# Pairwise products of fields: order of the pairs, PSUM operand, store sizes and the split of the last store

## The chip, the cores and the metric

The kernel runs on one core of one Trainium2 chip. The metric is the device time of one execution in microseconds (us); shorter is better. A profile shows one execution in detail; its span runs from the first to the last instruction of the program, and the device time includes a little on both sides of it.

## What is computed

```python
def ref(x, W):                      # x: (4096, 32, 64) float32, W: (64, 64) float32
    vid = einsum('bfd,de->bfe', x, W)
    idx_i, idx_j = triu_indices(32, k=1)
    return x[:, idx_i, :] * vid[:, idx_j, :]      # (4096, 496, 64)
```

For each of 4096 samples there are 32 fields of 64 numbers. Each field is multiplied by W, and each of the 496 pairs of fields i < j gives the elementwise product of field i as it came and field j after the multiplication. Input is 33.6 MB, output 520 MB, all float32.

## The kernel before, in words

The host lays x out as 16 tiles of shape 128 partitions x 32 fields x 128 samples: each of two groups of 128 samples takes 64 partitions, one for each of the 64 numbers. The output of a tile is 128 partitions x 496 pairs x 128 samples, so a pair is 512 bytes of a partition and 64 KB in all. The host puts the output into the reference's order afterwards.

For each tile, `project` (line 63) multiplies the fields by W on TensorE (line 72): a matmul takes four fields (one PSUM bank of 512 float32 columns) of one half of the partitions, and the compiler makes two instructions of each. ScalarE copies groups of eight fields from PSUM to an SBUF tile `vid` (line 79). `products` (line 82) walks over the left fields i: VectorE multiplies field i, broadcast, by the run of fields j after it (line 88). A tile's 496 pairs are cut into slots of 83 pairs (`SLOT`, line 34), with three slot buffers (line 46), and `store` (line 95) sends a slot to the output by a DMA on the queue of SP: six stores a tile, of which the last is 81 pairs. In tile 0 the pairs are made backwards, from the last left field, so that its first stores are small (lines 109 to 118): 10, 18, 27 and 26 pairs, then halves of slots.

Loads of x come in on SP for tiles 0 (four pieces of eight fields, last fields first) and 1 (two pieces of 16 fields). For later tiles they are four pieces on ScalarE's queue, called after a few stores of the tile before (lines 124 to 125). There are two x buffers, so the load of a tile waits until VectorE and TensorE have left the tile two earlier. W is loaded twice, once for each half of the partitions, on ScalarE's queue (lines 53 and 54). The order on SP is that of the program text; the framework adds the waits, and gives every DMA a semaphore that counts its landing.

Of the kernel before, what the change touches and what calls it, by code (L numbers as in the profile page):

```python
# [1 line left out]

# [4 lines left out]

F32 = mybir.dt.float32
ALU = mybir.AluOpType

P = 128

C = 128


@with_exitstack
def pairwise_bilinear_kernel(
    ctx: ExitStack,
    tc: tile.TileContext,
    x: bass.AP,  # L20
    w: bass.AP,
    out: bass.AP,
):

    nc = tc.nc
    NT, _, F, _ = x.shape
    D = P // 2
    NP = F * (F - 1) // 2

    GRP = 8  # L30
    NGRP = F // GRP
    BANK = 512 // C

    SLOT = 83
    AHEAD = 2
    PIECES = 4

    off = [i * (F - 1) - i * (i - 1) // 2 for i in range(F)]


    ctx.enter_context(tc.manual_schedule(engines={mybir.EngineType.SP}))

    const = ctx.enter_context(tc.tile_pool(name="const", bufs=1))
    xpool = ctx.enter_context(tc.tile_pool(name="x", bufs=AHEAD))
    vpool = ctx.enter_context(tc.tile_pool(name="vid", bufs=2))
    opool = ctx.enter_context(tc.tile_pool(name="out", bufs=3))
    psum = ctx.enter_context(
        tc.tile_pool(name="ps", bufs=4, space=bass.MemoryType.PSUM)
    )


    w2 = const.tile([P, D], F32)
    nc.scalar.dma_start(out=w2[0:D, :], in_=w)
    nc.scalar.dma_start(out=w2[D : 2 * D, :], in_=w)

    xs = {}

    def load(t, lo, hi, queue=nc.sync):
        if t not in xs:
            xs[t] = xpool.tile([P, F, C], F32, tag="x", name=f"x_{t}")  # L60
        queue.dma_start(out=xs[t][:, lo:hi, :], in_=x[t][:, lo:hi, :])

    def project(t, order):

        vid = vpool.tile([P, F, C], F32, tag="vid", name=f"vid_{t}")
        for g in order:
            pv = psum.tile([P, GRP, C], F32, tag="pv", name=f"pv_{t}_{g}")
            for b in range(0, GRP, BANK):
                f = g * GRP + b
                for h in range(2):  # L70
                    half = slice(h * D, (h + 1) * D)
                    nc.tensor.matmul(  # L72
                        pv[half, b : b + BANK, :],
                        lhsT=w2[half, :],
                        rhs=xs[t][half, f : f + BANK, :],
                        start=True,
                        stop=True,
                    )
            nc.scalar.copy(vid[:, g * GRP : (g + 1) * GRP, :], pv)  # L79
        return vid  # L80

    def products(t, vid, ot, base, a, b, backwards=False):

        fields = [i for i in range(F - 1) if off[i] < b and off[i + 1] > a]
        for i in reversed(fields) if backwards else fields:
            s, e = max(a, off[i]), min(b, off[i + 1])
            j = i + 1 + s - off[i]
            nc.vector.tensor_tensor(  # L88
                ot[:, s - base : e - base, :],
                xs[t][:, i : i + 1, :].to_broadcast([P, e - s, C]),  # L90
                vid[:, j : j + e - s, :],
                ALU.mult,
            )

    def store(t, ot, base, a, b):
        nc.sync.dma_start(out=out[t][:, a:b, :], in_=ot[:, a - base : b - base, :])


    for g in reversed(range(NGRP)):
        load(0, g * GRP, (g + 1) * GRP)  # L100
    load(1, F // 2, F)
    load(1, 0, F // 2)

    for t in range(NT):
        vid = project(t, reversed(range(NGRP)) if t == 0 else range(NGRP))
        bases = list(range(0, NP, SLOT))
        if t == 0:

            ends = [NP, off[27], off[24], off[21], bases[-1]]
            for n, base in enumerate(reversed(bases)):  # L110
                top = min(base + SLOT, NP)
                if n:
                    ends = [top, (base + top) // 2, base]
                ot = opool.tile([P, SLOT, C], F32, tag="o", name=f"o_{t}_{n}")
                for b, a in zip(ends, ends[1:]):
                    products(t, vid, ot, base, a, b, backwards=True)
                    store(t, ot, base, a, b)
        else:
            for n, base in enumerate(bases):
                top = min(base + SLOT, NP)  # L120
                ot = opool.tile([P, SLOT, C], F32, tag="o", name=f"o_{t}_{n}")
                products(t, vid, ot, base, base, top)
                store(t, ot, base, base, top)
                if 1 <= n <= PIECES and t + 1 < NT and t + 1 not in (0, 1):
                    load(t + 1, (n - 1) * F // PIECES, n * F // PIECES, nc.scalar)


_INS = ["r_x", "L0_rec_W"]
_OUTS = [((4096, 496, 64), "float32")]


# [28 lines left out]
```

## Time and profile before

| | |
|---|---|
| median of 4 runs | 1297.98 us (1297.72 to 1298.29) |
| the profiled execution's own time | 1297.76 us |
| its span | 1295.9 us |
| mean rate of the DMA over the span | 427 GB/s |
| HBM read, written | 33.59 MB, 520.09 MB |
| DMA engines' time taken by SP's queue, by ScalarE's | 93.9%, 5.6% |
| stores of 5312 KB: number, us from issue to landing | 75, 28.8 |
| x pieces of 512 KB on ScalarE's queue: number, us to landing | 56, 31.8 |
| TensorE clock granted, mean | 0.547 |

How to read it: PE is TensorE's matmuls and PEld its weight loads, DVE is VectorE, ACT is ScalarE, POOL is GpSimd, SP is SyncE. A group line gives source line, engine, operation, output and inputs, count, busy time and mean duration. In the rows of 40 slices a digit is the busy share in tenths of a 32 us slice. A row of a stretch gives, after its length, the busy time and count of PE, PEld, DVE, ACT and POOL, then the granted clock, the mean share in which the 16 DMA engines were busy, and GB/s. A line of waits gives who waited for whom, the total, the times and the longest, in us. A DMA is cut into packets, here one for each partition; each of the 16 engines works off its own share of them, and one of the landing counts is sent by each engine.

### The profile page before, as it was taken

What the parts mean: (1) busy time and instruction counts of PE and PEld (TensorE: products, weight loads), DVE (VectorE), ACT (ScalarE), POOL (GpSimd) and SP (SyncE); (2) the same over time, 40 slices, a digit from 0 to 9 for tenths busy, and PEclk for the clock granted to TensorE, in tenths of its full rate; (3) what the DMA queues carried; (4) which work ended last, traced back from release to release, by engine and by line L of the source; (5) the groups of instructions that cost most, each with busy time, mean ns of one, the idle gap of its engine ahead of it and who ended that gap; (6) DMA issues with size and microseconds to landing.
All of it is one profiled execution on the core that took longest, in us unless ns stands there. A gap on an engine that the chain in (4) does not pass through costs nothing.

```text
span 1295.9 us, 2185 instructions
## 1 busy us (share of the span) xinstructions
PE 217.4 (17%) x512; PEld 56.0 (4%) x512; DVE 1105.8 (85%) x581; ACT 66.1 (5%) x65; POOL 0.2 (0%) x4
## 2 busy tenths in 40 slices
PE   5013022120221302113031130311203122021000
PEld 2000000000000000000000000000000000000000
DVE  6999988889888888888888888888888888988991
ACT  2001000000000000000000000000000000000000
POOL 0000000000000000000000000000000000000000
PEclk9556566555555655556555555655556555565555
DMA  8999999999999999999999999999999999999997
GB/s 337 430 404 442 432 435 432 431 433 432 431 435 434 431 433 432 433 432 433 434 432 433 433 431 432 434 433 431 432 435 429 437 429 433 433 427 436 437 430 342
DMA packets 24076, 553.82 MB, mean 427 GB/s; under 512 B 2816, under 2 KB 2816, under 8 KB 10624
## 3 DMA queue, kind: packets, MB, share of 16 engines
q1 hardware_dynamic: 15840, 524.30, 93.9%
q10 hardware_dynamic: 8224, 29.40, 5.6%
q8 instruction: 4, 0.07, 0.0%
q14 instruction: 8, 0.07, 0.0%
HBM read 33.59 MB, written 520.09 MB: 427 GB/s over the span
## 4 chain that ended last, share of the span: by engine, by line
DMA 63%; DVE 33%; issue 1%; PE 0%; DVEq 0%; ACT 0%
DMA out_dram<-o 63%; DVE o L88 33%; DMA w<-in_L_rec_W_dram 0%; PE pv L72 0%; DVEq L154 0%; ACT vid L79 0%; DVEq L88 0%
## 5 line engine op out<-in xcount | busy, mean ns | idle before, releaser
L88 DVE TENSOR_TENSOR o<-x,vid 128x1408 f32<-128x1408 f32 (+15 forms) x581 | 1105.8, 1973 | 163.8 <-DMA out_dram<-o 152.9
L72 PE MATMUL pv<-x,w 64*64 64x512 f32 x512 | 217.4, 994 | 960.1 <-DMA x<-in_r_x_dram 954.8
L79 ACT COPY vid<-pv 128x1024 f32<-128x1024 f32 x64 | 64.8, 1012 | 1110.5 <-PE pv L72 998.7
L72 PEld LDWEIGHTS pv<-x,w 64*64 64x64 f32 x512 | 56.0, 204 | 1119.8 <-issue 1105.8
L79 ACT ACT_TABLE_LOAD x1 | 1.3, 1283 | 1.9 <-issue 1.9
L139 POOL MEMSET const-bfloat16-1.0<- 128x1 bf16 x1 | 0.1, 103 | 0.0
L139 POOL MEMSET const-uint8-127<- 128x1 uint8 x1 | 0.1, 102 | 0.0
L139 POOL MEMSET const-float32-0.0<- 128x1 f32 x1 | 0.1, 100 | 0.2 <-issue 0.2
L139 POOL MEMSET const-float32-1.0<- 128x1 f32 x1 | 0.1, 99 | 0.0
## 6 DMA issues: line engine op xcount, KB each, us to landing
out_dram<-o SPq DMA_DIRECT2D x75, 5312.0 KB, 28.8
out_dram<-o SPq DMA_DIRECT2D x15, 5184.0 KB, 27.7
x<-in_r_x_dram ACTq DMA_DIRECT2D x56, 512.0 KB, 31.8
out_dram<-o SPq DMA_DIRECT2D x5, 2688.0 KB, 10.2
out_dram<-o SPq DMA_DIRECT2D x5, 2624.0 KB, 10.8
x<-in_r_x_dram SPq DMA_DIRECT2D x4, 512.0 KB, 5.7
x<-in_r_x_dram SPq DMA_DIRECT2D x2, 1024.0 KB, 9.6
out_dram<-o SPq DMA_DIRECT2D x1, 1728.0 KB, 5.5
```

The source lines that it names most:

```text
L72: nc.tensor.matmul(pv[half, b : b + BANK, :], lhsT=w2[half, :], rhs=xs[t][half, f : f + BANK, :], start=True, stop=True,)
L79: nc.scalar.copy(vid[:, g * GRP : (g + 1) * GRP, :], pv)
L88: nc.vector.tensor_tensor(ot[:, s - base : e - base, :], xs[t][:, i : i + 1, :].to_broadcast([P, e - s, C]), vid[:, j : j + e - s, :], ALU ...
L139: nc = _bacc.Bacc("TRN2", target_bir_lowering=False, num_devices=1)
```

## The change

The order of the pairs, and with it the layout of the output in device memory, goes by right field: all pairs with j = 1, then j = 2, and so on; the pairs of a right field are consecutive (`first(j)` is where they start). The host's reordering follows. VectorE now multiplies a run of x fields by one right field, broadcast, and reads that field in PSUM, where the matmul left it. The copies by ScalarE and the tile `vid` in SBUF are gone. The eight PSUM banks hold the 32 fields of a tile, one bank for four fields.

A slot has 124 pairs, so that a tile has four; three buffers as before. A store goes out at the end of a slot, and over the first two tiles also at the sizes that `GROWING` lists: 26 stores that sum to 992 pairs. The last store of the last tile is cut by `steps`: first eight DMAs, each of 16 partitions, that leave out the last 1 to 8 pairs (one more for each group), then for each group two small DMAs for those pairs, one of 15 to 8 partitions and one of 1 to 8.

The host passes W already doubled, and one DMA on SP loads it before x. Tile 0 comes in four pieces, first fields first, tile 1 in two, later ones in four on ScalarE's queue, all called at the start of the tile before. The program is built with a smaller scratch area for DMA descriptors in SBUF (1024), which leaves room for the larger slots.

```diff
+SLOT = 124
+GROWING = [
+    21, 15, 19, 23, 27, 19, 29, 18, 19, 20, 38, 28, 24, 25, 47, 34, 29, 61,
+    55, 69, 66, 58, 77, 47, 93, 31,
+]
+def first(j):
+    return j * (j - 1) // 2
+def steps(lo, hi):
+    for g in range(8):
+        yield lo, hi - g - 1, 16 * g, 16 * g + 16
+    for g in range(8):
+        yield hi - g - 1, hi, 16 * g, 16 * g + 15 - g
+        yield hi - g - 1, hi, 16 * g + 15 - g, 16 * g + 16
...
-        tc.tile_pool(name="ps", bufs=4, space=bass.MemoryType.PSUM)
+        tc.tile_pool(name="ps", bufs=8, space=bass.MemoryType.PSUM)
...
-    nc.scalar.dma_start(out=w2[0:D, :], in_=w)
-    nc.scalar.dma_start(out=w2[D : 2 * D, :], in_=w)
+    nc.sync.dma_start(out=w2, in_=w)
...
+    def load(t, pieces, queue):
+        xt = xpool.tile([P, F, C], F32, tag="x", name=f"x_{t}")
+        n = F // pieces
+        for lo in range(0, F, n):
+            queue.dma_start(out=xt[:, lo : lo + n, :], in_=x[t][:, lo : lo + n, :])
+        return xt
+    loaded = [load(0, 4, nc.sync), load(1, 2, nc.sync)]
...
+    for t in range(NT):
+        if 0 < t < NT - 1:
+            loaded.append(load(t + 1, 4, nc.scalar))
+        xt = loaded[t]
+        vid = []
+        for b in range(0, F, BANK):
+            pv = psum.tile([P, BANK, C], F32, tag="pv", name=f"pv_{t}_{b}")
+            for h in range(2):
+                half = slice(h * D, (h + 1) * D)
+                nc.tensor.matmul(
+                    pv[half, :, :],
+                    lhsT=w2[half, :],
+                    rhs=xt[half, b : b + BANK, :],
+                    start=True,
+                    stop=True,
+                )
+            vid.append(pv)
-            nc.scalar.copy(vid[:, g * GRP : (g + 1) * GRP, :], pv)
...
+        sent = 0
+        for j in range(1, F):
+            i = 0
+            while i < j:
+                at = first(j) + i
+                base = at - at % SLOT
+                if at == base:
+                    ot = opool.tile([P, SLOT, C], F32, tag="o", name=f"o_{t}_{at}")
+                n = min(j - i, base + SLOT - at)
+                nc.vector.tensor_tensor(
+                    ot[:, at - base : at - base + n, :],
+                    xt[:, i : i + n, :],
+                    vid[j // BANK][:, j % BANK : j % BANK + 1, :].to_broadcast([P, n, C]),
+                    ALU.mult,
+                )
+                i += n
+                at += n
+                if t * NP + at == until or at in (base + SLOT, NP):
+                    last = t == NT - 1 and at == NP
+                    for lo, hi, p, q in steps(sent, at) if last else [(sent, at, 0, P)]:
+                        nc.sync.dma_start(
+                            out=out[t][p:q, lo:hi, :],
+                            in_=ot[p:q, lo - base : hi - base, :],
+                        )
+                    sent = at
+                    if t * NP + at == until:
+                        until += next(growing, NT * NP)
...
-    nc = _bacc.Bacc("TRN2", target_bir_lowering=False, num_devices=1)
+    nc = _bacc.Bacc("TRN2", target_bir_lowering=False, num_devices=1, dynamic_dma_scratch_size=1024)
...
+    w = _np.concatenate([w, w])
...
+    order = [first(j) + i for i in range(F) for j in range(i + 1, F)]
+    got = got.transpose(1, 0, 4, 3, 2)[:, :, :, order]
```

## The prediction, made before the changed kernel ran

> **What bounds it.** I read the page first, then stretches of the span with their DMA rate, then the waits of the SP queue.
>
> ```profile
> PE 217.4 (17%) x512; PEld 56.0 (4%) x512; DVE 1105.8 (85%) x581; ACT 66.1 (5%) x65; POOL 0.2 (0%) x4
> DMA  8999999999999999999999999999999999999997
> GB/s 337 430 404 442 432 435 432 431 433 432 431 435 434 431 433 432 433 432 433 434 432 433 433 431 432 434 433 431 432 435 429 437 429 433 433 427 436 437 430 342
> ```
>
> DVE is 85% busy, but the DMA row is full from the second slice to the last but one, at a rate that hardly moves. The program writes 520 MB and reads 34 MB, and the change alters none of these bytes. So the middle is a fixed cost, and only the ends can give anything. The stretches show where the ends leak:
>
> ```profile
> 0.00:13.00 13.00, 7.67 (x26) 4.09 (x28) 2.13 (x5) 3.31 (x3) 0.20 (x4) 1.00 0.84 320
> 13.00:50.00 37.00, 8.80 (x40) 4.71 (x36) 37.00 (x25) 6.08 (x6) 0.00 (x0) 0.68 0.91 385
> 50.00:100.00 50.00, 5.61 (x14) 1.63 (x16) 50.00 (x20) 1.01 (x1) 0.00 (x0) 0.50 1.02 421
> 100.00:1200.00 1100.00, 195.28 (x437) 45.54 (x434) 952.75 (x500) 55.67 (x55) 0.00 (x0) 0.54 1.00 433
> 1290.00:1296.00 6.00, 0.00 (x0) 0.00 (x0) 0.00 (x0) 0.00 (x0) 0.00 (x0) 0.50 0.05 21
> ```
>
> The last number of a row is GB/s. Against the steady 433, the stretch 13 to 50 loses (433-385)/433 x 37 = 4.1 us and 50 to 100 loses 12/433 x 50 = 1.4 us. In both, DVE (third busy figure) works without a pause: stores come too late because DVE starts only at 10.87 us and is hardly faster than the DMA. The stretch 0 to 13 loses 3.4 us, of which 1.8 pass before the first packet and the rest while the first reads get going. In the last stretch the share is 0.05, under one engine of 16: a single DMA engine works on alone. In the packets the others end at 1288.7 to 1291.5 us and that one at 1294.6; the last store's median landing is 1289.75, its last 1295.08. This straggler (5.3 us) has grown steadily since 450 us.
>
> ```profile
> SPq L96 <- DVE o L88: 1140.2, 103, 13.7
> SPq L96 <- DMA x<-in_r_x_dram: 82.0, 13, 12.4
> ```
>
> The second line looks odd: a store has no business waiting for a load of x. The instruction records explain it. All 168 DMAs of SP and ACT share eight semaphores in turn, and before each store SP waits for that semaphore's previous DMA to land. At 92.18 us the products of a store were done; it was issued at 92.70, just after the load eight DMAs earlier had landed at 92.64. **So at most eight DMAs are in flight.** This matters below.
>
> [...] pieces of x land 13.8 us apart beside 42.5 KB stores, that is 8 x (1571+159) ns. [...] No row of before has DVE read PSUM; from SBUF a product takes 75 to 80 ns + 133 ns a pair from start to start (208, 336, 468 ns for 1, 2, 3 pairs)[...].
>
> **The change, part by part**, against the profiled execution's own 1297.76 us (1.86 us outside its span; the median of the runs is 1297.98).
>
> Host-side order, the layout and the smaller scratch cost no device time. ACT's 64 copies (1.01 us each) go; ACT is not on the long chain after the first, so elsewhere that is worth nothing.
>
> *Start.* W moves ahead of x on SP, so the first x piece is issued 0.44 us later (one issue). Before, PE waited for W (5.29 us) and almost as long for x (5.11), then again for W's second half (6.67). I let PE start at 5.5. Its first bank now needs 4 matmul instructions, about 2.0 us at the cold pace of the trace, and no 1.0 us copy: DVE starts at about 7.5 instead of 10.87. A product from PSUM [...] bounds 0.08 (as SBUF) and 0.25. Fields 1 to 6 give the first 21 pairs at about 11.7; the loads keep the engines busy until 13.2. A pair then costs the DMA 0.151 us, and 0.87 us pass from products to first packet (DVE 15.17, packet 16.04). Running both clocks through the 26 first stores, the DMA is always later than the products, by 0.1 to 3 us, except at the 38-pair store (ready 44.3, engines free 45.2) and the 61-pair one (78.9 and 79.3), the tight ones: 0.5 us idle in all. At 0.08 it is 0, at 0.20 3.3, at 0.25 5.6. So: gain 4.1, new gaps 0.5. Of the 1.4 after 50, I take back 1.0: the store held for a semaphore at 92.7 and the drained queue behind it. The rest is loads, which move fewer bytes per time (4096 B in 155 ns).
>
> *Middle.* DMA bytes are the same. Packet times (309 ns for 8192 B, 1571 for 42496) give 0.0368 ns a byte and about 4 ns a packet. An engine's store packets fall from 832 to 672: -0.7 us. Were 63,488 B cut in two, it would be +1.1 instead; were they slower than the line through the smaller sizes, nothing here would show it. [...] two full stores (37 us) are queued while it fills a slot. Loads: 32 packets of an engine alternate with 32 store packets of 2.34 us, so x lands over 80 us, a whole tile. Its last piece (fields 24 to 31) is due only at pair 276, over 40 us later: nothing. The four ACT issues wait in a queue where nothing else stands. PE's next-tile matmuls wait for DVE to leave a bank, which happens field by field: nothing. Eight DMAs a tile over eight semaphores mean that stores wait for old stores and loads for old loads: nothing, covered by those two stores.
>
> *End.* The last slot now goes out as 8 groups of 16 partitions and then 16 small tails. By the split, engine 0 gets 36 pairs more than the mean and engine 15 gets 36 less: 36 x 512 B = 0.68 us. **But the ninth DMA must wait for the first.** Tail 8 waits until group 7 has landed on the slowest engine, that is until all the bulk is over. Then SP still has nine tails to issue: 332 ns each plus 104 ns for the wait and the gaps (the trace's issue, 45, 17 and 42 ns). The ninth starts 3.5 us later and needs 1.37 us (fixed part of the second and third stores: 4.15-2.78 and 5.52-4.15) + 0.16. That is +5.0, less 0.68 if the straggler is the engine that is spared: +4.3. No trace row shows a DMA of under 64 partitions: at 0.3 us each it is +3, at 0.6 us (W's issue on ACT took 0.55 to 0.61) +6; with no wait at all, -0.7. I take 4.3.
>
> Sum: 1297.76 - 4.1 - 1.0 + 0.5 - 0.7 + 4.3 = 1296.8 us.
>
> **Cases.** (0.2%, 2.6 us, is about what a measurement of this kernel can tell from no change.)
> A, 0.50: as above, 1296.8; its own range 1295.0 to 1299.6.
> B, 0.30: the tails don't queue up, because semaphores are given out otherwise or landings come early enough; then the straggler gets 0.68 us less and the time is 1296.8 - 4.3 - 0.7 = 1291.8. For it: the split aims at a real skew (1.6 us between first and 14th landing). Against it: the eight semaphores in turn.
> C, 0.16, the slower side: a product read from PSUM costs more. From 0.24 us fixed, DVE loses its lead over the growing stores, and the gaps come to 5.6 us at 0.25: 1296.8 + 5.1 = 1301.9. [...] For it: no row shows it, and the stores leave margins near zero.
> D, 0.04: 63 KB packets run apart from the line, or W first brings PE nothing, 1298.
>
> Faster: 0.28 of B and 0.09 of A's lower edge, 0.37. Slower: 0.15 of C and 0.02 of A. The rest is the same. A range of 1290.8 to 1300.4 leaves out C and the edges of B.
>
> **What would show it.** DVE's first product near 7.5 us; 13 to 50 us near 430 GB/s; [...] stores of 7936 KB; the median engine done some 6 us earlier than 1289.3. At the end, SP waits one by one behind its own stores, and the last 5 us have almost no bytes. The prediction is wrong if the 24 issues of the last store run through without waits, if the first 100 us keep gaps, or if the straggler has moved.

## The result and the profile after

The changed kernel takes 1323.02 us (median of 8 runs, 1318.68 to 1328.19) against 1298.19 of the kernel before beside it (11 runs): ratio 1.0194, 95% interval 1.0178 to 1.0211. The forecast was 1296.8, the range 1290.8 to 1300.4: wrong, and by more than any of the cases allowed. The profiled execution took 1320.77 us, with a span of 1318.9.

The page of the changed kernel: the engines' line, and the rows of DMA share and rate in 40 slices.

```profile
PE 226.8 (17%) x512; PEld 52.1 (4%) x512; DVE 1098.0 (83%) x544; POOL 0.2 (0%) x4
DMA  9999999999999999999999999999999999999995
GB/s 378 430 427 433 429 431 445 428 430 439 432 428 427 433 443 430 428 430 432 443 427 425 427 437 433 428 429 431 442 427 423 432 445 431 429 426 437 439 287 143
```

The first slice is better than before (378 for 337), as is the third (427 for 404). The two last slices fall to 287 and 143 GB/s, but the DMA row still says 9 in the first of the two: **the engines are busy and move little.** The stretches of the same kernel (the last two numbers of a row are the mean share in which the 16 DMA engines were busy, and GB/s) place it:

```profile
0.00:13.00 13.00, 6.63 (x20) 2.27 (x22) 3.99 (x7) 0.20 (x4) 1.00 0.83 303
13.00:50.00 37.00, 11.55 (x38) 2.56 (x34) 37.00 (x20) 0.00 (x0) 0.61 1.01 429
50.00:100.00 50.00, 7.62 (x16) 1.49 (x16) 50.00 (x28) 0.00 (x0) 0.53 1.01 428
100.00:1200.00 1100.00, 200.96 (x440) 45.83 (x440) 956.03 (x474) 0.00 (x0) 0.54 1.00 432
1200.00:1250.00 50.00, 0.00 (x0) 0.00 (x0) 45.57 (x17) 0.00 (x0) 0.50 1.00 432
1260.00:1270.00 10.00, 0.00 (x0) 0.00 (x0) 0.00 (x0) 0.00 (x0) 0.50 1.16 329
1270.00:1280.00 10.00, 0.00 (x0) 0.00 (x0) 0.00 (x0) 0.00 (x0) 0.50 1.00 188
1280.00:1290.00 10.00, 0.00 (x0) 0.00 (x0) 0.00 (x0) 0.00 (x0) 0.50 0.95 215
1290.00:1300.00 10.00, 0.00 (x0) 0.00 (x0) 0.00 (x0) 0.00 (x0) 0.50 0.83 206
1300.00:1310.00 10.00, 0.00 (x0) 0.00 (x0) 0.00 (x0) 0.00 (x0) 0.50 0.48 141
1310.00:1315.00 5.00, 0.00 (x0) 0.00 (x0) 0.00 (x0) 0.00 (x0) 0.50 0.09 26
```

Up to 1250 us little is slower: the first 13 us (303 GB/s for 320), and by a trifle the middle (432 for 433). From 13 to 50 us the rate is 429 for 385, from 50 to 100 it is 428 for 421. The damage lies behind 1260 us, in the last store: for 30 us the engines are busy at 0.83 to 1.00 and move about 200 GB/s, half of what the same engines moved at the same share before 1250. A packet of that store is slow, not waiting: the usual packet of 124 pairs (63,488 B) lasts 2.34 us in the middle (with such packets one after another 16 engines move 434 GB/s, and the middle moves 432), those of the last store's groups, which are a little smaller, had a median of 2.6 to 6.5 us, group by group, and lasted 13.6 us at most.

The SP queue's waits in the changed kernel (total, times, longest):

```profile
SPq L119 <- DVE o L108: 1168.5, 80, 22.0
SPq L119 <- DMA x<-in_r_x_dram: 49.1, 5, 19.0
SPq L119 <- DMA out_dram<-o: 47.0, 9, 22.6
```

The third line is new: SP waits behind its own stores, nine times. The records of the 24 issues say where. Seven groups go out from 1255.48 to 1263.3. The eighth waits until 1285.98, for the semaphore of the store eight DMAs earlier, which landed on its slowest engine at 1285.96. Then come the tails: the first at 1289.39, six more by 1311.47, each after a group's landing, and the last nine in a row behind the last group (1313.67), the final one landing at about 1318.1.

### The profile page after: what moved, and what is told of

The parts are those of the page before. It is cut to its first block, busy times and chain, and to the rows that moved or that the text cites. A ratio compares the mean times of both kernels' runs of the same rounds, so it can differ in the third digit from the quotient of the medians.

```text
span 1318.9 us, 2085 instructions
## 1 busy us (share of the span) xinstructions
PE 226.8 (17%) x512; PEld 52.1 (4%) x512; DVE 1098.0 (83%) x544; POOL 0.2 (0%) x4
## 4 chain that ended last, share of the span: by engine, by line
DMA 60%; DVE 33%; issue 1%; DVEq 0%; PE 0%; SPq 0%
DMA out_dram<-o 60%; DVE o L108 33%; DMA x<-in_r_x_dram 0%; DVEq L156 0%; PE pv L90 0%; DVEq L108 0%; SPq L65 0%
## 5 line engine op out<-in xcount | busy, mean ns | idle before, releaser
L108 DVE TENSOR_TENSOR o<-x,pv 128x2176 f32<-128x2176 f32 (+27 forms) x544 | 1098.0, 2092 | 157.4 <-DMA out_dram<-o 148.4
L90 PE MATMUL pv<-x,w 64*64 64x512 f32 x512 | 226.8, 1029 | 964.0 <-DMA x<-in_r_x_dram 885.3
L90 PEld LDWEIGHTS pv<-x,w 64*64 64x64 f32 x512 | 52.1, 208 | 1136.9 <-issue 1134.7
```

The lines of the kernel that those rows point to most:

```text
L90: nc.tensor.matmul(pv[half, :, :], lhsT=w2[half, :], rhs=xt[half, b : b + BANK, :], start=True, stop=True,)
L108: nc.vector.tensor_tensor(ot[:, at - base : at - base + n, :], xt[:, i : i + n, :], vid[j // BANK][:, j % BANK : j % BANK + 1, :].to_broad ...
```

## The experiments

The lag below is the time from the median to the last of a store's 16 landing counts; idle is the mean time that a DMA engine had no packet (packets at the median length for their size); the excess of packets is what they lasted beyond that length, as a sum per engine. Lags, idle times and excess are worked out from each run's single profile. Times are medians; edits are against the changed kernel if nothing else is said.

### 1. What the split of the last store costs

**e1_whole**: one DMA in place of the 24.

```diff
 def steps(lo, hi):
-    ...
+    yield lo, hi, 0, P
```

> The changed kernel with its last store sent as one DMA of 128 partitions, all else as changed. If the split of the last store is what costs [...], the time is 1296 to 1298 us, that of before or a little under. If the rest of the change (63 KB packets, PSUM operand) carries the loss, it stays near 1315 to 1320.

1298.66 us (12 runs), ratio 1.0001 (0.9993 to 1.0010). The split costs 24.4 us; everything else in the change comes to nothing on balance.

**e2_groups** keeps eight DMAs of 16 neighbouring partitions, without tails:

```diff
+    for g in range(8):
+        yield lo, hi, 16 * g, 16 * g + 16
```

> Last store as 8 DMAs of 16 neighbouring partitions with all their pairs, no small tails. [...] whole + about 18 us, near 1315, with packets of 63488 B far longer than 2.34 us at the end. Semaphore theory (only the chain of landings and issues costs): the chain has one link here, whole + 0 to 2 us.

1316.88 us (2 runs: 1313.70 and 1320.05), ratio 1.0144 (1.0116 to 1.0173): 18.2 over e1.

**e3_rows** also has eight DMAs, but cut by pairs, so that each has all 128 partitions:

```diff
+    cuts = [lo + (hi - lo) * g // 8 for g in range(9)]
+    for a, b in zip(cuts, cuts[1:]):
+        yield a, b, 0, P
```

> Last store as 8 DMAs too, but each of all 128 partitions and 15 or 16 pairs. [...] whole + 0 to 1 us. Semaphore theory, or a price for many DMAs: the same as with eight groups of partitions.

1298.58 us (18 runs), ratio 1.0004 (0.9997 to 1.0011). Eight DMAs in place of one cost nothing here; the way they are cut does. The same stretches of e1, then of e2:

```profile
1260.00:1270.00 10.00, 0.00 (x0) 0.00 (x0) 0.00 (x0) 0.00 (x0) 0.50 1.00 432
1270.00:1280.00 10.00, 0.00 (x0) 0.00 (x0) 0.00 (x0) 0.00 (x0) 0.50 0.98 425
1280.00:1290.00 10.00, 0.00 (x0) 0.00 (x0) 0.00 (x0) 0.00 (x0) 0.50 0.47 203
1290.00:1300.00 10.00, 0.00 (x0) 0.00 (x0) 0.00 (x0) 0.00 (x0) 0.54 0.06 25
```

```profile
1260.00:1270.00 10.00, 0.00 (x0) 0.00 (x0) 0.00 (x0) 0.00 (x0) 0.50 1.15 336
1270.00:1280.00 10.00, 0.00 (x0) 0.00 (x0) 0.00 (x0) 0.00 (x0) 0.50 0.98 229
1280.00:1290.00 10.00, 0.00 (x0) 0.00 (x0) 0.00 (x0) 0.00 (x0) 0.50 1.03 241
1290.00:1300.00 10.00, 0.00 (x0) 0.00 (x0) 0.00 (x0) 0.00 (x0) 0.50 0.87 190
```

A busy share of 0.98 carries 425 GB/s in e1 and 229 in e2. In e1 a low rate after 1280 goes with a low share: there the engines have nothing left. That is the difference between an engine that is idle and one that is held up, and the share alone doesn't show it.

### 2. Is it which partitions, or how few?

The changed kernel and e2 send the last store in DMAs of at most 16 partitions, all neighbours; in e1 and e3 each DMA has all 128. So either few partitions cost, or which they are. That neighbours are slow and partitions spread over the 128 are not was an assumption of mine, which no trace of before shows; the times expected of e2, e3, e4, e13 and e14 rest on it. An estimate from the rates of e1 and e2: the 8,126,464 B of the last store take 18.8 us at the 432 GB/s of e1 (1260 to 1270 us) and 35.5 at the 229 of e2 (1270 to 1280 us), so +16.7.

**e4_stride8**: eight DMAs of the partitions g, g+8, g+16 and so on: 16 in each as in e2, but spread over the 128.

```diff
+    for g in range(8):
+        yield lo, hi, g, P
...
-                            out=out[t][p:q, lo:hi, :],
-                            in_=ot[p:q, lo - base : hi - base, :],
+                            out=out[t][p : q : 8 if last else 1, lo:hi, :],
+                            in_=ot[p : q : 8 if last else 1, lo - base : hi - base, :],
```

> Last store as 8 DMAs of 16 partitions each, every eighth one (g, g+8, ...). [...] between whole and the 8 neighbouring groups, whole + 5 to 12 us. Semaphore theory, or a price for DMAs with one packet an engine: the same as with the neighbouring groups.

1314.01 us (2 runs), ratio 1.0122 (1.0102 to 1.0143): 15.4 over e1, more than I expected. Its slow packets collect at 4.0 to 5.2 us (95% of all are below 5.13; four lasted over 9 us), where those of e2 collect at 6 to 8 us and reach 9.24. Beside the usual 2.34 that is about half the rate in e4, and down to a quarter in e2. The time is nearly that of e2 all the same, and so is the rate: 222, 248 and 216 GB/s in the three stretches of 10 us from 1270 on, where e2 has 229, 241 and 190. Why every eighth partition still makes slow packets isn't shown.

**e13_stride4** and **e14_quarter** have four DMAs of 32 partitions each, the same packets and bytes. Only which partitions go together differs:

```diff
+    for g in range(4):
+        yield lo, hi, g, P                    # e13, with a step of 4 where e4 has 8
...
+    for g in range(4):
+        yield lo, hi, 32 * g, 32 * g + 32     # e14
```

> The changed kernel with its last store as four DMAs of 32 partitions, each of every fourth partition. [...] its packets stay at 2.34 us and it costs nothing, 1298.7. Rival (a DMA of few partitions is slow in itself): as much as e14, 1305 or more.

> The same with four DMAs of 32 neighbouring partitions[...] 5 to 16 us over the whole store: 1304 to 1315. Rival (few partitions are slow in themselves): the same time as e13, whichever that is.

e13: 1297.89 us (12 runs), ratio 0.9998 (0.9989 to 1.0006). e14: 1315.58 us (4 runs), ratio 1.0139 (1.0122 to 1.0156), just above the 1304 to 1315 that I expected. The stretches of e13, then of e14:

```profile
1260.00:1270.00 10.00, 0.00 (x0) 0.00 (x0) 0.00 (x0) 0.00 (x0) 0.50 1.00 432
1270.00:1280.00 10.00, 0.00 (x0) 0.00 (x0) 0.00 (x0) 0.00 (x0) 0.50 0.98 425
```

```profile
1260.00:1270.00 10.00, 0.00 (x0) 0.00 (x0) 0.00 (x0) 0.00 (x0) 0.50 1.12 330
1270.00:1280.00 10.00, 0.00 (x0) 0.00 (x0) 0.00 (x0) 0.00 (x0) 0.50 0.95 222
1280.00:1290.00 10.00, 0.00 (x0) 0.00 (x0) 0.00 (x0) 0.00 (x0) 0.50 1.04 286
```

In e13 all 206 packets that started after 1255 us lie between 2342 and 2356 ns; in e14 a quarter of them lasts 4.95 us or longer. With 32 partitions in each DMA of both, what costs is not the number of partitions, but which they are. Over e1 the three kernels with slow packets cost 18.2 (e2), 15.4 (e4) and 16.9 us (e14), near the 16.7 of the estimate. That e13 would cost nothing was expected before it ran (1298.7). What in the hardware divides these kernels is not shown: with other partitions a DMA reads other places in SBUF and also writes other rows of the output, and no run here changes one without the other. Nor does a DMA need all 128 partitions: e13, with 32 in each, moved 432 GB/s from 1260 to 1270 us.

### 3. The tails

**e9_tails**: one DMA over 128 partitions without the last 8 pairs, then 16 tails of 8 partitions for these.

```diff
+    yield lo, hi - 8, 0, P
+    for g in range(16):
+        yield hi - 8, hi, 8 * g, 8 * g + 8
```

> The changed kernel, but the bulk of the last store is one DMA over all 128 partitions without its last 8 pairs; these go as 16 tails of 8 partitions. What is left of the split are the tails that queue up for eight semaphores. Theory of the chain: nine tails cannot be issued before the bulk has landed, nine issues of about 0.34 us and one fixed part of 1.4 us end behind it, so 4 to 5 us over the kernel with a whole last store: about 1303, and the bulk itself runs at full rate. [...] Rival: the tails cost nothing, 1298.5.

1302.76 us (17 runs), ratio 1.0039 (1.0029 to 1.0049): 4.1 over e1. SP waits twice behind stores (total, times, longest):

```profile
SPq L117 <- DMA out_dram<-o: 32.8, 2, 20.4
```

Its records show it as predicted: one tail waits until 1278.72, for the store before; the next until 1299.447, when the bulk has landed on the last engine (1299.43). From there nine tails go out some 340 ns apart. (The profile is of the slowest of the 17 runs, 1306.60.)

### 4. Where the gain of the start went

In the changed kernel the engines' mean idle is 3.4 us at 100 us, before it was 7.6: the start has gained 4.2. But e1 ends where the kernel before ends. The table shows the last store's landing counts.

| | median landing, us | last landing, us | lag, us |
|---|---|---|---|
| before | 1289.75 | 1295.08 | 5.3 |
| e1_whole | 1284.07 | 1296.34 | 12.3 |
| e10_spload4 | 1289.05 | 1292.34 | 3.3 |

The median engine is 5.7 us earlier than before, as predicted ("some 6 us"), and the last one 1.3 us later. In its place a lag has grown, and it was there before the last store: in the changed kernel 1.5 to 2 us at 250, 3.8 at 460, 9.0 at 1246. It grows in steps, by store packets that last too long, most of the excess by 100 to 200 ns each, about one packet of a load (159 ns). The steps pile up on few engines: the last store of e1 lands on nine engines within 0.7 us, and on two of them 12.3 us after the median. How far it goes differs from profile to profile: with the same body and only the last store cut otherwise, the lag ahead of the end was 8.5 (e3), 10.0 (e13) and 12.8 (e9). From 100 to 1200 us the excess was 3.6 us per engine in the changed kernel, 2.8 in e1 and 0.8 before.

**e8_noload**: no loads after tile 1 (the later tiles use x of tiles 0 and 1 again).

```diff
-        if 0 < t < NT - 1:
-            loaded.append(load(t + 1, 4, nc.scalar))
-        xt = loaded[t]
+        xt = loaded[t % 2]
```

> Slots of 124, last store whole, and no load after tile 1: later tiles use the x of tiles 0 and 1 again, so their products are not those of the reference. The work falls by 14 x 4.97 us = 70 us an engine. If loads are what stretches store packets: hardly a packet of 63,488 B over 2.40 us, lag of the last landing under 3 us, time 1298.7 - 70 - 9 = 1220. If stores stretch each other: lag near 12 us and 1229.

1220.88 us (2 runs) for the expected 1220, lag 1.5 us, excess 0.8 us per engine. The lag comes with the loads.

**e5_slot83**, **e7_slot126** and **e6_load2** (all with a whole last store) change sizes:

```diff
-SLOT = 124
+SLOT = 83                                          # e5
...
-SLOT = 124
+SLOT = 126                                         # e7
...
-            loaded.append(load(t + 1, 4, nc.scalar))
+            loaded.append(load(t + 1, 2, nc.scalar))   # e6
```

> As changed, last store whole, but slots of 83 pairs as before (six stores a tile). Theory L (in the long stores of 63,488 B a partition the engines that lag get slower still, so two engines end 12 us late): the lag of the last landing behind the median falls from 12.3 us to about 5, the lag of before, and the time to 1291 to 1293, below both kernels. Rival N (the lag comes from PSUM operands, the ordering or the loads, whatever the slot): it stays at 1298.

> Slots of 126, 126, 126 and 118 pairs, last store whole: packets as long as with 124, but a store's rows no longer a quarter of an output row. If the length of packets is what matters: lag 12 us, 1298. If the regular addresses of 124 matter: lag near 5 us, 1292.

> Slots of 124, last store whole, loads of later tiles in 2 pieces of 8 KB a partition instead of 4 of 4 KB, so that load packets stand beside half as many store packets. If the stretching of store packets goes with the time in which loads are in flight, the lag of the last landing is about halved (6 us) and the time near 1293. If it goes with the slot alone, it stays at 12 us and 1298.

e5: 1300.84 us (12 runs), ratio 1.0022 (1.0013 to 1.0030), lag 7.5. e7: 1306.33 us (4 runs), ratio 1.0065 (1.0048 to 1.0082), lag 4.4. Both edits change more than the slot: the sizes in `GROWING` fit slots of 124 only. With 83 or 126 no product ends at pair 124, where the sixth store is due, so the list stops there and whole slots follow. The engines have been idle for 9.1 us in e5 and 19.0 in e7 at 150 us (3.3 in e1), and the times say nothing of the middle. The lags do not order by length of packet (7.5, 12.3 and 4.4 for 83, 124 and 126 pairs): the theory that long store packets make the lag finds no support. The other theory of e7, that the regular addresses of 124 pairs matter, has the lag right (near 5); with the start changed too, it is neither shown nor excluded. e6: 1301.53 us (7 runs), ratio 1.0035 (1.0022 to 1.0048), lag up to 20 and 16.4 at the end (the profile is of the slowest run, 1306.26). I expected fewer load packets to give less lag, and got more. One packet of a load now lasts 309 ns, and the stretches collect near 150, 300 and 450 ns, where in e1 nearly all were under 200: they have grown with the load's packet, but are not simply one of them.

**e10_spload4** puts the later loads into SP's own queue, behind the first store of a tile (whole last store):

```diff
-        if 0 < t < NT - 1:
-            loaded.append(load(t + 1, 4, nc.scalar))
...
                     sent = at
+                    if 0 < t < NT - 1 and at == SLOT:
+                        loaded.append(load(t + 1, 4, nc.sync))
```

> The changed kernel with a whole last store, and the loads of the tiles from 2 on issued on SP's own queue, four pieces behind the first store of a tile, so that an engine has no second queue to take turns with. Theory M: the stretched store packets, and with them the lag of the last engine, come from load packets of the other queue that run beside the stores; then the lag at the end falls from 12 us to 3 us or less, and the time to 1288 to 1291. Rival: the lag comes with the loads whichever queue they are in, 1298. Rival: a load behind a store is late for the next tile and DVE waits, over 1300.

1295.84 us (18 runs, 1295.00 to 1297.26), ratio 0.9984 (0.9977 to 0.9991). The lag is down to 3.3 us and the excess on the packets of whole slots to 0.4 us (e1: 2.4), as the theory of the two queues has it. The time is 5 us above the 1288 to 1291 that it gave. In the page of e10 all data is in one queue:

```profile
q1 hardware_dynamic: 20880, 553.69, 99.7%
GB/s 378 431 432 399 433 423 441 434 430 440 412 449 430 429 434 425 441 438 416 440 434 438 418 435 438 432 422 438 438 440 413 436 440 438 417 438 440 434 424 363
```

The fourth slice, with the first such load, has 399 GB/s (e1: 432); idle rises there from 3.2 to 5.5 us. Of the 512 reads of that load, between 109 and 117 us, 34 last 300 to 1400 ns and not 159. Over 100 to 1200 us the excess on load packets is 3.7 us per engine (e1: 0.1). So what was a lag of few engines in e1 has partly become a loss of all.

**e11_spload1** and **e15_later**: the same with one load of 16 KB a partition, and with the first such load one slot later.

```diff
-                        loaded.append(load(t + 1, 4, nc.sync))
+                        loaded.append(load(t + 1, 1, nc.sync))             # e11
...
-                    if 0 < t < NT - 1 and at == SLOT:
+                    if 0 < t < NT - 1 and at == (2 * SLOT if t == 1 else SLOT):  # e15
```

> The same with one load of 16 KB a partition in place of four pieces of 4 KB: 24 packets fewer for each engine and tile at about 4 ns each are 1.3 us less over 14 tiles. Theory M: 1287 to 1290. Rival (the load as one DMA keeps x back until all of it has landed, and DVE waits): over 1295. Rival (lag from the loads whichever queue): 1297.

> The kernel with loads in SP's queue (e10), with the load of the third tile one full slot later in the second tile. In e10 the DMA loses 2.3 us between 108 and 115 us, beside that load. If the loss comes from the load standing where the queue is thin, it goes: 1293.5. Rival: reads of that place in memory are slow whenever they run, 1295.8.

e11: 1299.57 us (20 runs, 1293.63 to 1303.20), ratio 1.0010 (0.9999 to 1.0020), lag 9.4: the theory is not enough, since with loads in larger packets the lag is back without a second queue. But it is another loss: the packets of whole slots have an excess of 0.5 us, as in e10, and the loads' own packets one of 5.2. e15: 1295.93 us (17 runs), ratio 0.9983 (0.9976 to 0.9990). The loss has moved with the load (idle rises from 3.1 to 5.3 us between 120 and 140), so a thin queue isn't the cause. The rival, a slow place in memory, doesn't hold either: e1 reads the same tile on ScalarE's queue, in 512 packets of which none lasts over 166 ns.

**e12_before_sp** was to do the same to the kernel before:

```diff
-                    load(t + 1, (n - 1) * F // PIECES, n * F // PIECES, nc.scalar)
+                    load(t + 1, (n - 1) * F // PIECES, n * F // PIECES, nc.sync)
```

> The kernel before, only its loads of later tiles moved from ScalarE's queue to SP's. Theory M: its lag of 5.3 us falls to about 2 us, so 1294 to 1295. Rival: the lag stays, 1298.

1414.06 us (4 runs), ratio 1.0896 (1.0880 to 1.0912). The waits in e12:

```profile
PE pv L72 <- DMA x<-in_r_x_dram: 1099.3, 56, 100.1
DVE o L88 <- ACT vid L79: 295.4, 15, 21.0
```

DVE waits 19.7 us in each tile for ScalarE's copies, these for PE, and PE for x. There the loads stand behind the second to the fifth store of a tile, and x comes later: PE's longest wait for it is 100.1 us, where before it was 71.0. In e10 they stand behind the first of four. A miss: it says nothing of the lag, since the DMA has gaps (share 0.93 and 390 GB/s from 100 to 1200 us, before 1.00 and 433), but it shows what a load's place in the stores' queue costs.

## Why the prediction was wrong, point by point

**The start was right, though not each term.** DVE's first product began at 8.39 us, not 7.5: PE started at 6.37, as the first piece of x landed at 6.24, and the first bank took the expected 2.0: its four matmul instructions, which overlap, have 1.06 to 1.11 us each on record (0.59 from 11.4 us on). I had 4.1 + 1.0 - 0.5 = 4.6 us of gain; the idle shows 4.2. By the rates against 433 the stretch from 13 to 50 us gained 3.8 and the next one 0.8, while the first 13 us lost 0.5, which the sum didn't have.

**The price of PSUM was too high, and case C with it.** The 0.5 us of new gaps rested on an estimate of mine for a product from PSUM, which no row of before shows. The groups by shape, before and after, with their mean ns:

```profile
L88 DVE TENSOR_TENSOR o<-x,vid 128x2688 f32<-128x2688 f32 x33 | 97.3, 2951 | 0.0
L88 DVE TENSOR_TENSOR o<-x,vid 128x640 f32<-128x640 f32 x32 | 26.3, 821 | 28.8 <-DMA out_dram<-o 28.8
```

```profile
L108 DVE TENSOR_TENSOR o<-x,pv 128x2688 f32<-128x2688 f32 x32 | 94.3, 2946 | 0.0
L108 DVE TENSOR_TENSOR o<-x,pv 128x640 f32<-128x640 f32 x32 | 26.1, 816 | 38.5 <-DMA out_dram<-o 38.5
```

A product with one operand in PSUM takes 5 ns less, and from start to start 732 ns against 736 for 640 elements (medians). For 1, 2 and 3 pairs it is 205, 331 and 465 ns, where before had 208, 336 and 468: PSUM costs nothing extra here. The step's result (0.5 us) was small and its error harmless.

**The middle's term was too small, and its neighbour failed.** At the median lengths for their sizes, all packets take 1283.2 us per engine in e1 and 1285.6 before: 2.4 us saved, not 0.7. The "about 4 ns a packet" doesn't follow from the two lengths named with it; they give 7.6 ns, or 1.2 us for 160 packets. With their true lengths the saving is only 1.1 us: stretched packets took the rest. DVE took 17.0 to 17.7 us to fill a slot in the changed kernel and the DMA 18.7 to send it (eight packets of 2.34 us an engine), so DVE stayed ahead. What failed beside it is the assumption that the straggler's 5.3 us stay: it stood in no sum, and in e1 the lag was 12.3. That is 7.0 us, and e1 is 6.2 above the 1292.5 that the sum gives without its end (1296.8 - 4.3). That the lag makes up these 6.2 is argued from this nearness, not shown.

**The end: the chain was right, and what stood in front of it was missed.** "The ninth DMA must wait for the first" is in the trace. From the last group's landing to the end of the last tail the chain took 4.5 us, where the sum had 5.0; alone, in e9, it costs 4.1 for a forecast of 4.3. But the sum took the bulk of the last store at full rate: "36 x 512 B = 0.68 us" was the only difference of the groups that it knew (an estimate too: no packet record here names its engine). In this step the prediction failed. Groups of 16 neighbouring partitions moved about half the rate (e2: 229, 241 and 190 GB/s in the stretches from 1270 to 1300 us, for 432 in the middle), and e2 puts that at 18.2 us. I had bounded the number and the order of the DMAs, but not the form that the trace of before doesn't show, a store of fewer than 128 partitions, except for its issue. The waiting of the eighth group and of the first tails belongs here: the store that the eighth group waits for landed on its slowest engine 19.1 us after the median, where the one before it took 9.0: seven of its last packets took 3.6 to 5.1 us for the usual 2.34, beside the groups' packets.

By medians: 1296.8, +6.2 for the lag, +18.2 for the groups in place of one DMA, and 6.1 for the tails from e2 to the changed kernel where 4.3 were in the sum: 1296.8 + 6.2 + 18.2 + 1.8 = 1323.0. That this is the measured time proves nothing, since the parts are the steps between the sum and the measured times. With only two runs of e2, 6 us apart, the split between its 18.2 and the last 6.1 is good to some 3 us.

**Open.** Why the lag grows to 9 to 13 us in this kernel and to 5.3 before, with the same number of load packets in both, isn't settled. It needs the loads (e8). The stretching of store packets needs them in a queue of their own: with the loads in SP's queue it is gone (e10, e11, e15). But then the load packets last longer, and with 16 KB packets this brings a lag of the same size (e11). That the store's length makes it has no support (e5, e7). Nor is it settled why loads in SP's queue, above all the first, read slowly.

**A version a little below both:** e10, the change without its split and with the loads in SP's queue, at 0.9984 (0.9977 to 0.9991) of the kernel before. It is a gain of some 2 us, within the 0.2% that I called "same", though the interval leaves out 1.

## What to carry to other kernels

When a DMA is cut by partitions, ask first which partitions stand together in a piece, and measure it: in this store groups of 16 and of 32 neighbours cost 18.2 and 16.9 us (e2, e14) and every eighth partition 15.4 (e4), while the cut by the free dimension or with a step of 4 cost nothing (e3, e13: 1298.58 and 1297.89 us for the 1298.66 of e1). A busy share near 1 with half the rate was the sign of engines that are held up, and the share alone didn't show it. And a gain for the median engine is worth only what the last engine takes over of it: put the straggler's lag into the sum as a term with bounds of its own.

## What the runs showed that I had not expected

- The same packet takes more or less time by which partitions the store's DMAs put together: 63,488 B took 2.34 us in e13, in e4 mostly 4 to 5 us where it was stretched, and up to 9.2 in e2.
- Shorter packets need not make the store shorter: the stretched packets of e4 collect at 4.0 to 5.2 us and those of e2 at 6 to 8, and the two take 1314.01 and 1316.88 us.
- The busy share can pass 1 (1.16 from 1260 to 1270 us in the changed kernel): the view counts a packet whole in the stretch in which it starts. In these 10 us 16 packets were open for 9.4 us, and never more than 18.
- The times of one kernel can spread with the loads: e11 took 1293.63 to 1303.20 us, e10 only 1295.00 to 1297.26. That this is the lag is likely, but each has only one profile.
- With 4 KB pieces in a second queue stretched store packets collect near 150 ns too long, with 8 KB pieces near 150, 300 and 450; a packet of the load lasts 159 and 309 ns.
